# Four layers on one core: where a batch's last signs and its layer 3 stand among the next batch's scores

## The chip, the cores and the metric

The kernel runs on one core of a Trainium2 chip. The metric is the device time of one execution in microseconds (us). Three runs of the kernel before gave 1948.09, 1948.43 and 1948.29 us, median 1948.29. The profile is one more execution, of 1948.69 us, in which the engines' work spans 1946.8 us.

## The reference, cut to what matters

The input x has 8 batches of 512 channels and 32 x 32 = 1024 positions. Four layers follow one another, each with a residual.

```python
# layer 0: linear attention through 64 channels; sigma is a largest singular value
f, g = relu(batchnorm(Wf x)), relu(batchnorm(Wg x));  h = Wh x
x = Wv ((f^T g) / sigma  h^T) + x
# layer 1: group norm, softmax attention over 512 channels
h = group_norm(x);  a = softmax(q(h)^T k(h) / sqrt(512))
x = x + Wp (a v(h))
# layer 2: softmax attention over 128 channels
x = bn(Z (softmax(t(x)^T p(x) / sqrt(128)) g(x))) + x
# layer 3: product of signs
s = bn(sign(W) * scale @ sign(x + bias)) + x
out = prelu(s - shift) + bias
```

In layer 3 each batch's signs are a 512 x 1024 matrix of +1 and -1, multiplied by a 512 x 512 matrix of signs and then passed through a few elementwise operations.

## The kernel before, in words

**Stages.** A first section reads all batches for the batch norms of layer 0 and folds weights together; among them wu, so that u = wu h takes the place of q and k, and the scores of layer 1 are h^T u. Then `fast` (line 823) runs once for each batch, n = 0 to 7. A batch's 1024 positions are cut into two halves of 512 (`half`), its 512 channels into four chunks of 128 partitions. The steps of `fast` are:

1. `scores1`: the scores of layer 1 and their exponentials, in four rounds of seven products;
2. `make_v`: the values of layer 1, in two rounds of seven products;
3. `values1`: attention times values, 14 groups of products, added to x by GpSimd; on its way the next batch is normalised (`normal`, `split_h`);
4. `project2`, `scores2` and `values2`: layer 2. Between their products stand those of `make_u`, which makes the next batch's u, handed out one at a time by `fill`;
5. `close2` (line 654) for each half: layer 2's result is added to x by VectorE (L660);
6. `leave` (line 662) for each half: layer 3.

**Seven products.** The large products go through `seven` (line 318), a scheme that takes seven products of quarters instead of eight, with sums of quarters prepared beforehand. The factor on one side is cut into A11, A12, A21, A22 with sums S1 to S4, the other into B11 to B22 with T1 to T4. In the scores A is u and B the normalised batch h; S1, S2, S4 lie in the tile us, and S3 takes the place of A21 in ut. VectorE makes these sums when the last quarter of u is there (`sums_of`, lines 301 to 304: S1, S2, S3, S4 in this order). `seven` is a generator that stops after each product:

| stop | product | what follows it |
|---|---|---|
| 0 | A11·B11 into a bank pa | ACT copies it out (L335) |
| 1 | S2·T2 | VectorE adds the copy (L330) |
| 2 | S3·T3 | VectorE adds (L330) |
| 3 | S1·T1 into a bank pc | ACT copies it out (L324, or L326 with a bias), GpSimd adds (L345) |
| 4 | A12·B21 on top of pa | ACT moves it (L326), in the scores with exp (L351) |
| 5 | S4·B22 on top of pc | VectorE adds (L330, or L332 with a bias) |
| 6 | A22·T4 on top of S3·T3 | VectorE adds (L330, or L332 with a bias) |

`scores1` runs four such rounds, so its loop in `fast` counts k = 0 to 27; k = 0, 1, 2 are A11·B11, S2·T2, S3·T3 of the first round. Partial sums lie in eight PSUM banks that are handed round (`bank`).

**Layer 3.** `leave` does for a half: four signs on ACT (L668, one of 128 x 512 for each chunk, into the tile sg, fp16), then for j = 0 and 1 four products (L678) into a bank. The weights pack two sign matrices into one fp16 number, so ACT and VectorE take the result apart (L689, L690, L691). Then, for two outputs: L697 on VectorE adds x, L701 and L702 on ACT, L709 on VectorE, and SyncE sends 128 x 512 numbers out (L712). The generator stops after each j. The first half's `leave` runs in the same call of `fast`, with the next u's products in between. The second half's is put into the list `rest3` and taken up in the next batch's scores at odd k: at k = 1 the signs and j = 0, at k = 3 j = 1, at k = 5 its end, at which x of the batch after the next is asked for (`load_x`, L137) into the buffer that has become free.

**The chain.** `chain` (line 925) finds sigma for a pair of batches by repeated squaring of 128 x 128 matrices. Three such chains of 24 steps are spread behind the main work: `chore(2)` runs one step at every second stop of `scores1`, `make_v` and `values1`, so 14 + 7 + 7 steps in a batch, until all 72 are done, which is in n = 2. A step is two products (L938, L939) and their eviction, in turn by ACT (L952) and by VectorE; the steps of the latter kind also take a sum over partitions (L972) of the step before, which VectorE turns into a factor (L973, L999, L1000) before it evicts with that factor (L960) and prepares the next sum (L966, L967). A chain's end takes a logarithm and an exponential on ACT (L1010, L1013, each with a load of a table).

**What sets the order.** The program isn't executed in the order of the Python text. A scheduler in the layer that builds it orders the queue of each engine by the traced order, by what each instruction needs, and by costs that it assumes. In the built program of before, one of the two matmuls of A12·B21 stands in front of S2·T2, and the four signs of the second half stand on ACT behind L335 of the first round. Each engine then works through its queue in order.

Of the kernel before, what the change touches and what calls it, by code (L numbers as in the profile page):

```python
# [23 lines left out]
NH = N // HF  # L24
# [59 lines left out]
def kernel(  # L84
# [36 lines left out]
    def bank():  # L121
        return psum["bank"].tile([P, HF], F32, tag="bank", name="bank")
# [9 lines left out]
    def load_x(b, split=False):  # L132
        t = xpool.tile([P, CC, N], F32, tag="x", name="xt")
        src = x[b].rearrange("(cc p) n -> p cc n", p=P)
        for cc in range(CC):
            for ns in [half(h) for h in range(NH)] if split and not cc else [slice(0, N)]:
                nc.sync.dma_start(out=t[:, cc, ns], in_=src[:, cc, ns])  # L137
        return t

    def half(i):  # L140
        return bass.ts(i, HF)
# [73 lines left out]
    def col(name, i):  # L215
        return ct[:, COL[name] + i : COL[name] + i + 1]
# [234 lines left out]
    def split_h(env, ht):  # L451
        hs = env["big"].tile([P, 3, 2, HF], F32, tag="hs", name="hs")
        b = [ht[:, chunks[k], half(n)] for k in range(2) for n in range(2)]
        return differences_of(b, [hs[:, i] for i in range(3)])
# [199 lines left out]
    def close2(xt, att, h):  # L654

        for oc in range(CC):
            ps = bank()
            mm(out=ps, lhsT=sbw["z"][:, bass.ts(oc, P)], rhs=att, start=True, stop=True)  # L658
            xs = xt[:, oc, half(h)]
            nc.vector.tensor_tensor(xs, ps, xs, ALU.add)  # L660

    def leave(env, xt, dst, halves=range(NH), signs=None):

        small = env["small"]
        for h in halves:
            sg = env["e"].tile([P, CC, HF], F16, tag="e", name="sg")
            for cc in range(CC):
                nc.scalar.activation(  # L668
                    sg[:, cc, :], xt[:, cc, half(h)], AF.Sign, bias=rb3[:, cc : cc + 1]
                )  # L670
            for j in range(CC // 2):
                both = env["e"].tile([P, 2, HF], F32, tag="e", name="both")
                y1, y2 = both[:, 0, :], both[:, 1, :]

                def product(lt):
                    ps = bank()
                    for cc in range(CC):
                        mm(  # L678
                            out=ps,
                            lhsT=lt[:, cc, bass.ts(j, P)],  # L680
                            rhs=sg[:, cc, :],
                            start=cc == 0,
                            stop=cc == CC - 1,
                        )
                    return ps

                if signs is None:
                    ps = product(sw3)
                    nc.scalar.activation(y2, ps, AF.Identity, bias=round3, scale=1.0 / PACK)  # L689
                    nc.vector.tensor_scalar(y2, y2, ROUND, None, ALU.subtract)  # L690
                    nc.vector.scalar_tensor_tensor(y1, y2, -PACK, ps, ALU.mult, ALU.add)  # L691
                    sums = y1, y2
                else:
                    sums = [product(lt) for lt in signs]

                for y, ps, oc in ((y1, sums[0], j), (y2, sums[1], j + 2)):
                    nc.vector.scalar_tensor_tensor(  # L697
                        y, ps, sa3[:, oc : oc + 1], xt[:, oc, half(h)], ALU.mult, ALU.add
                    )
                    up = small.tile([P, HF], F32, tag="half_a", name="up3")  # L700
                    nc.scalar.activation(up, y, AF.Relu, bias=cb3[:, oc : oc + 1])  # L701
                    nc.scalar.activation(  # L702
                        y,
                        y,
                        AF.Identity,
                        bias=pb3[:, oc : oc + 1],
                        scale=col("L3_conv_pr_slope", oc),
                    )
                    nc.vector.scalar_tensor_tensor(  # L709
                        y, up, ps3[:, oc : oc + 1], y, ALU.mult, ALU.add  # L710
                    )
                    nc.sync.dma_start(out=dst[:, oc, half(h)], in_=y)  # L712
                yield
# [91 lines left out]
    def entering(n):  # L805

        b = order[n]
        f = load_f(b)

        def steps():  # L810
            while b // 2 not in ready:
                next(behind)
            if b % 2 == 0:
                for i in (b, b + 1):
                    pvs[i] = weights0(i)
            yield from enter(resident[b], f, pvs.pop(b))

        return steps()

    rest3 = []  # L820
    verdict = []

    def fast(env, n, hb, ua):


        b = order[n]
        xt = resident.pop(b)
        more = n + 1 < B
        ahead = iter(())
        count = [0]  # L830

        def chore(every):
            count[0] += 1
            if count[0] % every == 0:
                next(behind, None)

        es = [None] * NT
        for k, _ in enumerate(scores1(env, hb, ua, es)):
            if rest3 and k % 2:
                if next(rest3[0], "end") == "end":  # L840
                    rest3.pop()
                    if more and order[n + 1] not in resident:
                        resident[order[n + 1]] = load_x(order[n + 1])
            if k == 8 and more:
                ahead = entering(n + 1)
            if k >= 11 and k % 3 == 0:
                next(ahead, None)
            chore(2)
        for _ in ahead:
            pass  # L850
        esum = es.pop()
        vt = env["big"].tile([P, NT, C], F32, tag="uv", name="vt")
        for k, _ in enumerate(make_v(hb, vt)):
            if k == 3:
                r = inverse_sums(env, esum, n)
            chore(2)
        scratch = env["big"].tile([P, 3, N], F32, tag="us", name="scratch")
        got = []
        steps = iter(())
        for k, _ in enumerate(values1(env, xt, vt, es, r, scratch)):  # L860
            chore(2)
            if k == 5 and more:
                nxt = resident[order[n + 1]]
                hb = split_h(env, normal(env, nxt))
        signs = None
        if more:
            steps = make_u(env, hb, got)
        else:
            signs = unpacked(env)

        def fill(k=1):
            for _ in range(k):
                next(steps, None)

        made = []
        for k, _ in enumerate(project2(env, xt, made)):
            fill(k > 5)
        tt, pt, gt = made
        es, esum = scores2(env, pt, tt, lambda t: fill(t % 2))
        banks, r = [None, None], None  # L880

        def values2(h, ts):
            if banks[h] is None:
                banks[h] = bank()
            for t in ts:
                mm(  # L886
                    out=banks[h],
                    lhsT=gt[:, t, :],
                    rhs=es[t][:, half(h)],
                    start=t == 0,  # L890
                    stop=t == NT - 1,
                )
            if t == NT - 1:
                att = env["small"].tile([P, HF], F32, tag="half_b", name="att")
                nc.vector.tensor_tensor(att, banks[h], r[:, h, :], ALU.mult)
                return att

        dst = channels(out[b])  # L900
        fill()
        values2(0, range(0, 2))
        r = inverse_sums(env, esum, B + n)
        values2(0, range(2, NTH))
        att = values2(0, range(NTH, NT))
        values2(1, range(0, NTH))
        close2(xt, att, 0)
        att = values2(1, range(NTH, NT))
        count = iter(()) if more else count_bad(env)
        next(count, None)  # L910
        fill()
        for _ in leave(env, xt, dst, [0], signs):
            fill()
        close2(xt, att, 1)
        fill(2)
        for _ in steps:
            pass
        rest3.append(leave(env, xt, dst, [1], signs))
        if not more:
            for _ in rest3.pop():  # L920
                next(count, None)

        return hb, got[0] if more else None
# [111 lines left out]
    env = {}  # L1035
# [105 lines left out]
    for b in range(B):  # L1141
        xt = load_x(b) if b else first
# [361 lines left out]
    with tc.If(verdict[0] > 0):  # L1504
        with (
# [5 lines left out]
            env = {"big": big, "e": epool, "small": small}  # L1511
# [4 lines left out]
            for b in range(B):  # L1516
                xt = load_x(b)
# [43 lines left out]
```

## Time and profile before

| what | from the profile |
|---|---|
| span | 1946.8 us, of which the first section to the first u takes about 227 |
| one batch, scores to scores, n = 1 to 2 | 450.18 to 679.66 us |
| one batch, scores to scores, n = 3 to 4 | 900.67 us to 1113.09 us |
| matmul 128x512 fp32, two records | 0.86 us from one to the next |
| one sign product 128x512 fp16 | 0.21 us from one to the next |
| L668 sign on ACT | 0.72 us mean |
| chain of work that ended last | PE 93%, DVE 3%, ACT 2% |
| clock granted to TensorE | 0.997 |

In the lines of the page a product of fp32 is counted twice (its two passes), so x4 means two matmuls. A bracket at the end of a line of the time line gives the idle time of the engine before it and what ended it. PE's busy time overlaps from one matmul to the next, so the distance between two starts, not the duration, is what a matmul costs.

### The profile page before, as it was taken

The numbers are of one execution on the slowest core, as the hardware profiler recorded it, in microseconds if no ns is written. First come the engines' busy times: TensorE is split into PE (matmuls) and PEld (weight loads), VectorE is DVE, ScalarE is ACT, GpSimd is POOL, SyncE is SP. The second block draws the span as 40 slices with busy tenths as digits, with TensorE's granted clock in tenths as the row PEclk, the third lists the DMA queues.
The fourth block names the chain that finished last, engine by engine and source line by source line (L and its number), as shares of the span: only waits on it lengthen the run. The fifth ranks groups of instructions, "written<-read, shape, count | busy, mean of one in ns | idle before, by whom it ended". The sixth has DMA issues, their size and how long they took to land.

```text
span 1946.8 us, 16715 instructions
## 1 busy us (share of the span) xinstructions
PE 1908.0 (98%) x6230; PEld 982.9 (50%) x6230; DVE 1149.2 (59%) x1867; ACT 514.4 (26%) x815; POOL 223.6 (11%) x176
## 2 busy tenths in 40 slices
PE   8999999999999999999999999999999999999997
PEld 3367456544655446454555446544645455544653
DVE  3255577447864687537754677348663775466545
ACT  2141221134221342025212331034202421134014
POOL 1000001200112001200111011200120011101120
PEclk9999999999999999999999999999999999999999
DMA  8320000002000110002000120002000200010001
GB/s 322 147 76 7 1 6 12 1 11 87 17 1 0 33 65 17 1 8 85 17 5 1 33 71 12 1 11 87 11 0 1 73 26 10 0 33 22 11 0 56
DMA packets 27289, 67.00 MB, mean 34 GB/s; under 512 B 3824, under 2 KB 4592, under 8 KB 26560
## 3 DMA queue, kind: packets, MB, share of 16 engines
q1 hardware_dynamic: 26112, 65.09, 9.7%
q8 instruction: 51, 0.84, 0.2%
q0 software_dynamic: 224, 0.33, 0.1%
q10 hardware_dynamic: 864, 0.43, 0.1%
q14 instruction: 38, 0.31, 0.1%
HBM read 38.51 MB, written 18.87 MB: 29 GB/s over the span
## 4 chain that ended last, share of the span: by engine, by line
PE 93%; DVE 3%; ACT 2%; issue 0%; DMA 0%; ACTq 0%; POOL 0%; DVEq 0%
PE bank L373 43%; PE bank L540 20%; PE bank L886 6%; PE bank L764 6%; PE bank L1151 4%; PE bank L641 3%; PE bank L658 3%; PE bank L396 2%; PE wide L1191 1%; PE bank L678 1%; PE bank L938 1%; PE bank L939 1%; PE bank L785 1%; PE wide L1238 1%; DVE st L408 0%; ACT up L701 0%
## 5 line engine op out<-in xcount | busy, mean ns | idle before, releaser
L540 PE MATMUL bank<-e,vt 128*128 128x512 f32 x768 | 334.0, 593 | 0.0
L540 PEld LDWEIGHTS bank<-e,vt 128*128 128x128 f32 x768 | 145.0, 190 | 175.4 <-issue 173.2
L373 PE MATMUL bank<-ut,h 128*128 128x512 f32 x384 | 183.3, 598 | 4.7 <-ACT e L335 4.7
L330 DVE TENSOR_TENSOR e<-bank,e 128x512 f32<-128x512 f32 x128 | 87.7, 685 | 61.4 <-PE bank L373 60.2
L373 PE MATMUL bank<-us,hs 128*128 128x512 f32 x256 | 121.3, 596 | 0.5 <-DVE us L302 0.5
L373 PEld LDWEIGHTS bank<-ut,h 128*128 128x128 f32 x384 | 70.6, 190 | 87.7 <-issue 73.5
L886 PE MATMUL bank<-e,tpg 128*128 128x512 f32 x256 | 114.6, 595 | 0.0
L764 PE MATMUL bank<-tpg 128*128 128x512 f32 x256 | 114.6, 592 | 0.0
L771 ACT ACTIVATE e<-bank 128x512 f32<-128x512 f32 x128 | 76.4, 597 | 128.5 <-PE bank L764 128.5
L373 PE MATMUL bank<-h,wu 128*128 128x512 f32 x192 | 90.7, 594 | 2.2 <-ACT ut L335 1.5
L373 PE MATMUL bank<-wo,h 128*128 128x256 f32 x384 | 91.9, 382 | 0.0
L345 POOL TENSOR_TENSOR e<-e 128x512 f32<-128x512 f32 x32 | 41.6, 1300 | 432.3 <-ACT e L324 361.3
L776 DVE TENSOR_TENSOR esum<-esum,e 128x1024 f32<-128x1024 f32 x48 | 58.8, 1225 | 54.9 <-ACT e L771 54.9
L330 DVE TENSOR_TENSOR vt<-bank,vt 128x512 f32<-128x512 f32 x64 | 44.0, 688 | 69.5 <-PE bank L373 69.3
L886 PEld LDWEIGHTS bank<-e,tpg 128*128 128x128 f32 x256 | 48.0, 190 | 63.9 <-issue 63.9
L764 PEld LDWEIGHTS bank<-tpg 128*128 128x128 f32 x256 | 48.6, 190 | 60.8 <-issue 60.5
L373 PEld LDWEIGHTS bank<-wo,h 128*128 128x128 f32 x384 | 71.5, 190 | 14.3 <-ACT vt L324 4.9
L345 POOL TENSOR_TENSOR ut<-ut 128x512 f32<-128x512 f32 x16 | 21.8, 1360 | 483.0 <-ACT ut L326 483.0
L373 PEld LDWEIGHTS bank<-us,hs 128*128 128x128 f32 x256 | 47.3, 190 | 57.5 <-issue 51.4
L793 DVE RECIPROCAL rsum<-bank 128x512 f32<-128x512 f32 x16 | 53.7, 3356 | 30.3 <-PE bank L785 30.3
L668 ACT ACTIVATE sg<-xt,rb 128x512 f16<-128x512 f32 x64 | 43.8, 717 | 103.7 <-DVE xt L660 100.9
L1151 PE MATMUL bank<-xt,fg 128*64 128x512 f32 x256 | 59.3, 608 | 4.5 <-DMA fg<-in_w_fg 4.5
(320 smaller groups left out, 3076.3 us busy)
## 6 DMA issues: line engine op xcount, KB each, us to landing
xt<-in_x SPq DMA_DIRECT2D x55, 512.0 KB
out<-both SPq DMA_DIRECT2D x64, 256.0 KB
rfull<-rsum SPq DMA_DIRECT2D x64, 128.0 KB
f_dram<-f SPq DMA_DIRECT2D x8, 256.0 KB
fb<-f_dram SPq DMA_DIRECT2D x8, 256.0 KB
w<-in_w SPq DMA_DIRECT2D x1, 1024.0 KB
q<-in_w_q SPq DMA_DIRECT2D x1, 1024.0 KB
k<-in_w_k SPq DMA_DIRECT2D x1, 1024.0 KB
```

Source lines behind the costliest of these rows:

```text
L330: nc.vector.tensor_tensor(dst, ps, u, ALU.add)
L345: nc.gpsimd.tensor_tensor(c22, c22, c12, ALU.add)
L373: mm(out=ps[:, q * w : (q + 1) * w], lhsT=lt(ka, kb, q, k), rhs=rhs(ka, kb, q, k), start=first and q == 0 and k == 0, stop=last and k == 1 ...
L540: mm(out=ps, lhsT=a[:, t, bass.ts(r_, P)], rhs=e[t], start=first and t == 0, stop=last and t == NTH - 1, skip_group_check=True,)
L641: mm(out=ps[:, i, :], lhsT=xt[:, cc, bass.ts(4 * h + i, P)], rhs=sbw["tpg"][:, cc, 2 * P : 3 * P], start=cc == 0, stop=cc == CC - 1,)
L658: mm(out=ps, lhsT=sbw["z"][:, bass.ts(oc, P)], rhs=att, start=True, stop=True)
L764: mm(out=ps, lhsT=pt[:, 0, bass.ts(t, P)], rhs=tt[:, 0, half(h)], start=True, stop=True,)
L771: nc.scalar.activation(e[:, half(h)], ps, AF.Exp, scale=float(P) ** -0.5)
L776: nc.vector.tensor_tensor(esum, esum, e, ALU.add)
L793: nc.vector.reciprocal(r, ps)
L886: mm(out=banks[h], lhsT=gt[:, t, :], rhs=es[t][:, half(h)], start=t == 0, stop=t == NT - 1,)
L1151: mm(out=banks[i][side(h), :], lhsT=w0[i][:, cc, :], rhs=xt[:, cc, half(h)], start=cc == 0, stop=cc == CC - 1,)
```

## The change

`leave` gets an argument that makes it stop once more, after the signs. In `fast` the second half's `leave` is made before the last products of the next u are traced, and, if there is a next batch, its signs are traced there at once. In the next scores layer 3 is taken up at even k: j = 0 at k = 0, j = 1 at k = 2, its end (and `load_x`) at k = 4. As long as it runs, `chore` isn't called, so the two chain steps at k = 1 and k = 3 fall away there and all later steps come two later; this concerns n = 1 and n = 2 (in n = 0 there is no layer 3 left over, and from n = 3 on no chain).

```diff
-    def leave(env, xt, dst, halves=range(NH), signs=None):
+    def leave(env, xt, dst, halves=range(NH), signs=None, stop=False):
...
                     sg[:, cc, :], xt[:, cc, half(h)], AF.Sign, bias=rb3[:, cc : cc + 1]
                 )
+            if stop:
+                yield
             for j in range(CC // 2):
...
         for k, _ in enumerate(scores1(env, hb, ua, es)):
-            if rest3 and k % 2:
+            if rest3 and k % 2 == 0:
                 if next(rest3[0], "end") == "end":
                     rest3.pop()
...
-            chore(2)
+            if not rest3:
+                chore(2)
         for _ in ahead:
             pass
...
         close2(xt, att, 1)
+        rest3.append(leave(env, xt, dst, [1], signs, more))
+        if more:
+            next(rest3[0])
         fill(2)
         for _ in steps:
             pass
-        rest3.append(leave(env, xt, dst, [1], signs))
```

In the built program the queues hold the same instructions as before, in other places. At the start of the scores PE's queue reads A11·B11, the four sign products of j = 0, S2·T2, S3·T3, the four of j = 1, S1·T1, A12·B21; no half of A12·B21 is pulled ahead. On ACT the first of the four signs stands before the last L702 of the first half, two more before the last L326 of u, the fourth behind it and before L335. On SyncE the first transfer of x stands ahead of the two outputs of j = 1 and the second between them.

## The prediction

> **What bounds the kernel now.** I read the page first, then the list of who waited for whom on PE, then the time lines of PE, DVE and ACT around those waits. Batches are numbered n = 0 to 7 in the order they run.
>
> ```profile
> span 1946.8 us, 16715 instructions
> PE 1908.0 (98%) x6230; PEld 982.9 (50%) x6230; DVE 1149.2 (59%) x1867; ACT 514.4 (26%) x815; POOL 223.6 (11%) x176
> ```
>
> PE is busy for 98% and the granted clock is 9 tenths or more in every slice, so only idle PE time can be won. PE's waits in the whole span add up to some 26 us; two of the larger ones recur:
>
> ```profile
> PE bank L373 <- ACT e L335: 4.7, 7, 0.7
> PE bank L938 <- DVE cur L960: 3.9, 3, 1.8
> PE bank L416 <- DVE mv L415: 3.5, 5, 1.8
> ```
>
> (us in total, times, longest.) The first comes once in each of n = 1 to 7, the 1.8 us ones of the second once in n = 1 and once in n = 2. The third has one wait of 1.8 us before the main loop and four of 0.4 us late in the scores. Here is PE in n = 1, where the scores begin (start, duration):
>
> ```profile
> 450.18 1.88 PE L373 MATMUL bank<-ut,h 128*128 128x512 f32 x4
> 452.73 1.13 PE L373 MATMUL bank<-ut,h 128*128 128x512 f32 x2 [0.68 <-ACT e L335]
> 453.70 1.88 PE L373 MATMUL bank<-us,hs 128*128 128x512 f32 x4
> 455.41 1.03 PE L678 MATMUL bank<-sg,sw 128*128 128x512 f16 x4
> ```
>
> Every fp32 matmul is shown as two records. A pair (x4) is issued in 1.72 us elsewhere in this stage, four f16 products in 0.86. The first line is A11·B11; the second is half of A12·B21, pulled ahead while S2 isn't ready, and it must wait for ACT to copy A11·B11 out of the same bank. From 450.18 to the end of the sign products at 456.28 pass 6.10 us for 1.72 + 0.86 + 1.72 + 0.86 = 5.16 us of work: **0.94 us lost**, and n = 3 has the same 6.10 (900.67 to 906.77). What S2·T2 really needs is the second of DVE's sums:
>
> ```profile
> 449.96 1.23 DVE L301 TENSOR_TENSOR us<-ut 128x1024 f32<-128x1024 f32 x1
> 451.10 0.75 DVE L332 SCALAR_TENSOR_TENSOR ut<-bank,bu,ut 128x512 f32<-128x512 f32 x1
> 451.76 1.22 DVE L302 TENSOR_TENSOR us<-us,ut 128x1024 f32<-128x1024 f32 x1
> ```
>
> It ends at 452.98, 2.80 after 450.18. At n = 0, where nothing is pulled ahead, PE starts S2·T2 at 229.25, 0.05 after L302's end. ACT meanwhile:
>
> ```profile
> 446.05 0.81 ACT L702 ACTIVATE both<-both,pb,ct 128x512 f32<-128x512 f32 x1
> 446.95 0.69 ACT L326 ACTIVATE ut<-bank,bu 128x512 f32<-128x512 f32 x1
> 452.10 0.58 ACT L335 COPY e<-bank 128x512 f32<-128x512 f32 x1 [4.46 <-PE bank L373]
> 452.58 2.56 ACT L668 ACTIVATE sg<-xt,rb 128x512 f16<-128x512 f32 x4
> ```
>
> It idles 4.46 us, and the four signs come only afterwards. The second wait, in n = 1:
>
> ```profile
> 466.65 1.88 PE L373 MATMUL bank<-ut,h 128*128 128x512 f32 x4
> 470.34 0.46 PE L938 MATMUL bank<-cur 128*128 128x128 f32 x2 [1.81 <-DVE cur L960]
> ```
>
> ```profile
> 467.28 0.15 DVE L973 COPY tr<-bank 128x1 f32<-128x1 f32 x1
> ...
> 468.25 0.75 DVE L709 SCALAR_TENSOR_TENSOR both<-up,ps,both 128x512 f32<-128x512 f32 x1
> ...
> 469.65 0.54 DVE L960 TENSOR_SCALAR cur<-bank,r 128x256 f32<-128x256 f32 x1
> ```
>
> The chain's eviction L960 stands in DVE's queue behind layer 3's L690 to L709. PE was free at 466.65 + 1.72 = 468.37: 1.97 us idle, plus 0.07 for the slower restart (470.34 to 470.63 instead of 0.22): **2.04 us lost**, and the same in n = 2 (697.86 to 699.83).
>
> **What the Trainium skill says.** "PSUM — Partial Sum Buffer", Engine vs sequencer instructions: ACT, DVE and GpSimd queues are strict FIFO and matmuls start in program order. The trace agrees: L960 waits its turn above. Same page, PSUM bank collisions: a bank must not be written by PE while ACT reads it; agrees: PE goes on at 452.73, 0.05 after the copy's end at 452.68. "GPSIMD Engine Reference", Specifications: GpSimd shares SBUF interfaces with DVE instructions of two SBUF inputs or in a 2-port mode; agrees: L709, 0.74 alone, took 1.17 beside POOL's L345, and L690, 0.43 alone, 1.12. "ScalarE: Activation LUTs", What ACT_TABLE_LOAD costs: 1.283 us plus a drain of 1.38; the trace has 1.28 with the activation right behind (544.02, then 545.31), so 1.28 is used.
>
> **The change, part by part.** The queues of the built program show no instruction added or removed; only places change. T is the start of A11·B11.
>
> 1. Signs. ACT gets its four L668 (0.62 apart) before L335: the first before the last L702, two more before the last L326, the fourth after it. The x halves leave DVE's L660 at 445.73, 447.41, about 448.0 and 449.3. So sign 1 ends at 446.65, L702 at 447.35, signs 2 and 3 at 448.8, L326 at 449.4 (447.64 before), sign 4 at 450.0. Who is queued behind: L326, which the second matmul of A11·B11 (451.04) and L302 (451.76) need, and L709, which needs L702 and moves one L660 back on DVE. None is late, so DVE's L302 keeps 452.98. This costs nothing; ACT's 4.46 us gap hides it.
>
> 2. PE at the start of the scores. New order: A11·B11, sign products j=0, S2·T2, S3·T3, sign products j=1, S1·T1, A12·B21, and so on. Sign products run T+1.72 to T+2.58 (their bank is released by the second L332, 451.85 + 0.05 = T+1.72). S2·T2 starts at T+2.85. Loss 0.27 + 0.10 restart = 0.37 instead of 0.94: **gain 0.57, seven times: 4.0**. S3 (L303) is ready at T+3.98 and wanted at T+4.67. Bounds: 0.27 if the restart doubles and L302 slips 0.2; 0.67 if no restart cost shows.
>
> 3. Layer 3 behind it. DVE: L304 to T+5.08, L690, L330 of S2·T2, L691, L330 of S3·T3 (from T+6.66), L697 twice (first ends T+8.0), then L690, L691, L697 for j=1 to T+10.4. ACT: L689 twice (second ends T+8.14), L701 twice, L702 twice to T+10.9, L701 to T+11.5, then the copy L324 of S1·T1's bank to **T+12.0**. PE wants that bank for S4·B22 at T+2.85+1.82+1.72+0.86+1.72+1.72+1.72 = **T+12.4**; in n = 1 and 2 three chain matmuls (0.58) stand before it. It is just in time: cost 0, bound 0 to 0.4 a batch.
>
> 4. Chain. Steps at k = 1 and 3 of n = 1 and 2 fall away there and come later, four in all. Two products and one total run after A12·B21 (from T+10.74 in n = 1), when DVE has mostly done layer 3; its L960 then ends near T+14.8, and the next chain matmul stands at T+16.5, behind A22·T4, S4·B22 and the next A11·B11 (5.2 us of PE work; in n = 1 before it was 2.7). The stall goes: **2 x 2.04 = 4.1**. Bounds 0 (moved) to 4.1. Other steps keep their parity, so the 0.31 wait at 490.79 stays.
>
> 5. The moved steps. Their PE time is the same work elsewhere. In n = 1 the second chain now ends in the value stage: its trace sum must pass DVE's L446 x2, L330, L312, L562, L313, L563, L573 (0.66 to 1.5 each). From the stage's start V I get its L967 at V+6.8, PE wants it at V+6.9. I charge **0.2**; bounds 0 and 1. Two table loads (2.56) move onto ACT where it has only copies some 3 us apart; nobody on PE waits for these. POOL's L984 falls behind two L579 (5.05 for both) and holds DVE's L985 for up to 2 us; DVE idles 14 us of 50 in that stage and PE's operands for the next two groups are done. In n = 2 the third chain ends at the sixth step of the v stage, where the second did in n = 1 without a wait.
>
> 6. SP. x for the next batch is asked for at k = 4 instead of 5, its first transfer ahead of j=1's two outputs, the second between them. Before, loads started at T+15.9 (916.54) and DVE's first use at T+28.7 (929.40) waited for PE's bank, not for a transfer; the new last load is issued near T+16. Nothing.
>
> Sum: 4.0 + 4.1 - 0.2 = **7.9 us** of the 1946.8 us span: 1938.9. The timed runs lie 1.5 above this span (median 1948.29): **1940.4**.
>
> **Rivals.**
> (a) The chain stall moves instead of going: gain 4.0 - 0.2 = 3.8, 1944.5. For: the chain still crosses a busy DVE (POOL's L345 from T+12.1 slows L709 there). Against: 1.7 us of slack in step 4.
> (b) S4·B22 waits for L324, about 0.6 a batch, and eats the gain of step 2: 4.1 - 0.2 - 0.2 = 3.7, 1944.6. For: the margin is 0.4 us, on a sum of a dozen durations.
> (c) Slower: the same copy L324 is far late, because the L701 before it needs DVE's L690, L691, L697 of j=1, which stand behind j=0's. It decides from a wait of 7.9 / 7 = 1.1 us a batch, slower by 0.2% from 1.7; at 2.2 it gives 1940.4 + 15.4 = 1955.8. DVE would have to run 2.6 us later than I sum; nothing there takes that long, so it is unlikely.
> (d) No effect: the built queues exclude it.
>
> **How the numbers follow.** A measurement of this kernel can tell about 0.2% (3.9 us) from no change. Forecast 0.68 (its own range 1939.3 to 1942), (a) 0.14, (b) 0.14, (c) 0.04. (a) and (b) lie on the edge of 0.2%, half of each counts as faster: faster 0.81, same 0.15, slower 0.04. Range: down to 1939.0 (step 2 at 0.67, step 5 at 0: 8.8, with the runs' spread), up to 1944.4, just short of (a) and (b).
>
> **What would show it.** In the profile after: PE's wait for ACT L335 gone, replaced by some 0.3 us for DVE L302 seven times; ACT's L668 before L335; sign products right after A11·B11; no 1.81 us wait for L960; a wait for tj L967 in n = 1's value stage of 0.2 us. Wrong would be a wait of L373 for ACT e L324 near T+12, a wait for L960 near T+16, or L302 later than T+2.9.

## The result and the profile after

The changed kernel took 1939.49 us in the median of four runs (1938.61 to 1942.25), the kernel before 1948.19 in the median of four (1948.06 to 1948.43). The ratio is 0.9958, with a 95% interval of 0.994 to 0.9975: some 8.2 us faster by the ratio, 8.7 us between the medians. In the changed file the lines are 1 to 6 higher than before: the signs are L669, layer 3 is L681 and L692 to L712, the chain's products are L944 and L945, its eviction L966, its sum L978, and L973 gives tj.

The page's first lines, and from PE's list of waits (for whom: us in total, times, longest) the rows that answer to those shown above:

```profile
span 1940.4 us, 16698 instructions
...
PE 1909.5 (98%) x6230; PEld 984.6 (51%) x6230; DVE 1149.8 (59%) x1867; ACT 513.6 (26%) x815; POOL 224.1 (12%) x176
```

```profile
PE bank L416 <- DVE mv L415: 3.5, 5, 1.8
...
PE bank L373 <- DVE us L302: 0.5, 1, 0.5
...
PE bank L944 <- DVE cur L966: 0.3, 1, 0.3
```

The row of seven waits for the copy L335 is gone. Of the three waits for the chain's eviction only the one of 0.3 is left. The row for L302 is that of n = 0, as before. PE's time line in n = 1 (start, duration):

```profile
451.92 1.88 PE L373 MATMUL bank<-ut,h 128*128 128x512 f32 x4
453.63 1.03 PE L681 MATMUL bank<-sg,sw 128*128 128x512 f16 x4
454.77 1.98 PE L373 MATMUL bank<-us,hs 128*128 128x512 f32 x4
456.59 1.88 PE L373 MATMUL bank<-ut,h 128*128 128x512 f32 x4
...
464.13 1.88 PE L373 MATMUL bank<-us,h 128*128 128x512 f32 x4
...
468.43 0.39 PE L944 MATMUL bank<-cur 128*128 128x128 f32 x2
```

T is 451.92. The sign products end at 453.63 + 0.86 = 454.49, and S2·T2 starts at 454.77, T+2.85. The gap of 0.28 has no bracket, since the profile lets the sign products end at 454.66, only 0.11 before: so short a gap is seen only in the distance of the starts. S2·T2 then takes 1.82 to the next start instead of 1.72. The line at 464.13 is S4·B22, that at 468.43 the chain's next product, T+16.51, without a wait. ACT and DVE beside it:

```profile
447.67 0.71 ACT L669 ACTIVATE sg<-xt,rb 128x512 f16<-128x512 f32 x1
...
449.18 1.34 ACT L669 ACTIVATE sg<-xt,rb 128x512 f16<-128x512 f32 x2
450.43 0.67 ACT L326 ACTIVATE ut<-bank,bu 128x512 f32<-128x512 f32 x1
451.04 0.72 ACT L669 ACTIVATE sg<-xt,rb 128x512 f16<-128x512 f32 x1
...
463.21 0.56 ACT L324 COPY e<-bank 128x512 f32<-128x512 f32 x1
```

```profile
453.50 1.22 DVE L302 TENSOR_TENSOR us<-us,ut 128x1024 f32<-128x1024 f32 x1
...
466.14 0.54 DVE L966 TENSOR_SCALAR cur<-bank,r 128x256 f32<-128x256 f32 x1
467.20 0.74 DVE L712 SCALAR_TENSOR_TENSOR both<-up,ps,both 128x512 f32<-128x512 f32 x1
```

The signs are done at 451.76, before T. L302 ends at 454.72, T+2.80, where it ended before. L324 ends at T+11.85, 0.36 ahead of S4·B22. L966 ends at T+14.76.

**How the runs are compared.** Up to S2·T2 of n = 0, PE's first product that waits for L302 in the main loop, both kernels do the same. That section ended at 229.25 in the profile of before and at 230.99 in that of after, so the two spans hide 1.74 us (the last section returns to this). Below, the time from there to the end of the span is called the window. The span is given to 0.1 us, so a window is good to 0.05. The distance between the L302 of one batch and the next gives the batches:

| kernel | gate on chain steps | signs | layer 3 at k | window | n = 1 | n = 2 | n = 3 |
|---|---|---|---|---|---|---|---|
| before | no | behind | odd | 1717.55 | 229.49 | 221.01 | 212.42 |
| after | yes | ahead | even | 1709.41 | 225.92 | 219.52 | 211.86 |
| e1 | yes | behind | odd | 1715.78 | 226.31 | 222.40 | 212.43 |
| e2 | yes | ahead | odd | 1715.74 | 226.31 | 222.40 | 212.42 |
| e3 | yes | behind | even | 1713.45 | 226.46 | 220.09 | 212.41 |
| e4 | no | ahead | even | 1709.51 | 226.87 | 218.40 | 211.86 |
| e5 | no | behind | even | 1716.10 | 228.79 | 220.31 | 212.42 |

A window comes from one profiled execution each. The batches of kernels with the same order agree within 0.02 (n = 3 of before, e1, e2, e3 and e5), so in a batch a difference of a tenth can be read. A window is coarser: the stretch from VectorE's last result to the end of the span, in which the last results are sent out, takes 5.1 to 5.5 us over these profiles, also where the order is the same (5.2 in after, 5.4 in e4, which are alike from n = 3 on). After's window is 8.14 shorter than before's: n = 1 and 2 together 5.06, n = 3 to 6 by 0.56 to 0.60 each, and what follows the L302 of n = 7 by some 0.8, of which 0.3 lies behind VectorE's last result (5.4 in before). Without that 0.3 the gain is 7.9. Where chain steps move between n = 1 and n = 2, only their sum counts. The run times are coarser still: in the later series the kernel before took between 1945.88 and 1952.34 us, so the narrow range of its first four runs is no measure of the noise.

### The profile page after: what moved, and what is told of

Read it like the earlier page. It is cut to its first block, busy times and chain, and to the rows that moved or that the text cites. A ratio compares the mean times of both kernels' runs of the same rounds, so it can differ in the third digit from the quotient of the medians.

```text
span 1940.4 us, 16698 instructions
## 1 busy us (share of the span) xinstructions
PE 1909.5 (98%) x6230; PEld 984.6 (51%) x6230; DVE 1149.8 (59%) x1867; ACT 513.6 (26%) x815; POOL 224.1 (12%) x176
## 4 chain that ended last, share of the span: by engine, by line
PE 89%; DVE 8%; ACT 1%; issue 1%; DMA 0%; ACTq 0%; POOL 0%; DVEq 0%
PE bank L373 40%; PE bank L540 20%; PE bank L890 6%; PE bank L767 6%; PE bank L1157 4%; PE bank L641 3%; PE bank L396 2%; PE bank L658 1%; PE wide L1197 1%; PE bank L944 1%; DVE both L712 1%; DVE both L700 1%; PE bank L945 1%; PE bank L788 1%; PE wide L1244 1%
## 5 line engine op out<-in xcount | busy, mean ns | idle before, releaser
L330 DVE TENSOR_TENSOR e<-bank,e 128x512 f32<-128x512 f32 x128 | 87.7, 685 | 65.2 <-PE bank L373 64.5
L330 DVE TENSOR_TENSOR vt<-bank,vt 128x512 f32<-128x512 f32 x64 | 44.1, 689 | 70.5 <-PE bank L373 70.1
L669 ACT ACTIVATE sg<-xt,rb 128x512 f16<-128x512 f32 x64 | 45.2, 718 | 104.4 <-DVE xt L660 100.9
```

What stands on the lines that cost most here:

```text
L330: nc.vector.tensor_tensor(dst, ps, u, ALU.add)
L669: nc.scalar.activation(sg[:, cc, :], xt[:, cc, half(h)], AF.Sign, bias=rb3[:, cc : cc + 1])
```

## The experiments

**Which part gives what: e1 to e5.** The change has three edits: the gate (no chain step while layer 3 is pending), the signs traced ahead, and layer 3 at even k. Each ratio below is to the kernel before, with its 95% interval; differences of windows are to before where no other kernel is named. The signs ahead alone weren't run. e1 is the kernel before with the gate alone:

```diff
-            chore(2)
+            if not rest3:
+                chore(2)
```

> Only the gate on the chain steps: signs and layer 3 stay where they are before the change (signs behind the copy L335, layer 3 at odd k). By the theory on record the two parts of the gain are separate: the boundary loss of 0.94 us stays in n = 1 to 7 (the seven waits of PE for ACT's L335, 4.7 us together, are still in the list), the two 1.8 us waits for the chain's eviction are gone, 4.1 - 0.2 = 3.9 us: about 1944.3 against 1948.2. Rival (the stall only moves to the next chain matmul): within 1 us of 1948.2.

Measured: ratio 0.9988 (0.9981 to 0.9995), window 1.77 shorter. The seven waits for L335 are all there, as expected, but the chain gave 1.8 and not 3.9. Three smaller waits have come in; the first in n = 1, the others later in n = 2:

```profile
468.97 0.46 PE L939 MATMUL bank<-cur 128*128 128x128 f32 x2 [0.36 <-DVE cur L961]
...
745.81 0.46 PE L939 MATMUL bank<-cur 128*128 128x128 f32 x2 [0.42 <-DVE cur L961]
...
772.97 0.35 PE L973 MATMUL bank<-tj,mask 128*128 128x1 f32 x2 [0.56 <-DVE tj L968]
```

With their restarts they come to some 2.0 us, while the wait of 0.31 that before has at 490.79 is gone; the rest of the 2.1 that are missing isn't assigned. So with the gate alone the two waits of 1.8 are gone, but in n = 1 the eviction still stands behind layer 3's last result (0.36), and other waits have come in. This is not quite the gate of the change either: at odd k layer 3 is pending until k = 5, so the first chain step of a batch comes at k = 6. From the L302 of n = 1 to the next, 24 chain evictions are executed, against 27 in before and 25 in after, and n = 2 begins with one by ACT where before and after have one by VectorE.

e2 is the changed kernel with one edit undone:

```diff
-            if rest3 and k % 2 == 0:
+            if rest3 and k % 2:
```

> The signs ahead and the gate, but layer 3 still at odd k. In the built queue PE again has half of A12*B21 and then S2*T2 in front of the sign products, as before the change. If the boundary gain needs the sign products in front of S2*T2 (the theory), the loss there stays 0.94 and the gain is the chain's alone, 3.9: 1944.3. If ACT's signs standing behind the copy were the cause by themselves (rival), the gain is 7.9: 1940.3.

Measured: ratio 0.9987 (0.998 to 0.9994), window 1715.74, the same as e1 to 0.04, with the same waits and the same longer gate. Signs ahead are worth nothing as long as half of A12·B21 and S2·T2 stand in front of the sign products.

e3 is the changed kernel with the signs left where they were (the lines that put `leave` into `rest3` as before, no `next` there).

> Layer 3 at even k and the gate, but the signs not ahead: they stand behind the copy L335 on ACT. Theory: the sign products now have to wait for signs that end at about T+3.2, 3.8, 4.4 and 5.1 (T the start of A11*B11; in the trace of before the copy ends at T+2.5 and signs follow 0.62 apart), PE has 5.16 us of work to do until then and 0.2 of products behind the last sign; loss 0.9 to 1.2, so nothing is gained at the boundary: 3.9 or a little less, 1944.3 to 1946. Rival (even k alone is enough): 7.9, 1940.3.

Measured: ratio 0.9981 (0.9973 to 0.9989), window 4.10 shorter. The boundary loses what it lost before (212.41 in n = 3), the sign products now standing among S2·T2's matmuls, behind the wait for L335 as before; the chain's 1.8 us waits are gone. With e2, this shows that signs ahead and even k give the boundary's gain only together.

e4 is the changed kernel without the gate:

```diff
-            if not rest3:
-                chore(2)
+            chore(2)
```

> Everything of the change except the gate: the chain steps stay at k = 1 and 3. The step on record credits the chain's 4.1 us to the steps that fall away; then the 1.8 us waits stay and the gain is 4.0: 1944.2. Rival, which the built queue of VectorE speaks for: with layer 3 at even k the chain's eviction stands in front of the last layer-3 results, at about T+9.5 by a sum of durations, and PE has the next chain product only near T+11; then the stall goes without the gate and the gain is about 8: 1940.2.

Measured: ratio 0.9954 (0.994 to 0.9967), window 1709.51. This is the whole gain without the gate, so the rival is right. n = 1 and 2 together take 445.27, 0.17 less than in after. DVE in n = 1 (T = 449.52), and PE there:

```profile
458.71 0.54 DVE L965 TENSOR_SCALAR cur<-bank,r 128x256 f32<-128x256 f32 x1
459.16 0.75 DVE L712 SCALAR_TENSOR_TENSOR both<-up,ps,both 128x512 f32<-128x512 f32 x1
...
464.50 0.54 DVE L965 TENSOR_SCALAR cur<-bank,r 128x256 f32<-128x256 f32 x1
464.96 1.40 DVE L712 SCALAR_TENSOR_TENSOR both<-up,ps,both 128x512 f32<-128x512 f32 x2
```

```profile
460.02 0.39 PE L943 MATMUL bank<-cur 128*128 128x128 f32 x2
...
467.14 0.39 PE L943 MATMUL bank<-cur 128*128 128x128 f32 x2
```

Both evictions go in front of layer-3 results, and PE comes for them at 460.02 and 467.14, 0.8 and 2.1 us after they end.

e5 is the kernel before with layer 3 at even k alone (the edit of e2 the other way round), to see whether even k is the whole cause.

> The kernel before with one edit: layer 3 of the second half at even k; no gate, signs behind the copy. Theory formed from the earlier runs (the gate gives nothing; even k alone takes the chain's stall away; the boundary needs signs ahead and even k together): the two 1.8 us waits are gone, the seven 0.7 us waits for L335 stay, the time from S2*T2 of n = 0 to the end falls by 4.1 us from 1717.55 to about 1713.4, a little under the run with the gate (1713.45). Rival (the gate is needed as long as the signs stand behind): 1715.5 to 1717.5.

Measured: ratio 0.9996 (0.9988 to 1.0005), window only 1.45 shorter. By its run times it can't be told from before. The theory written for it falls, and the window lies where the rival has it: half of the stall is still there, in n = 1 and again in n = 2.

```profile
471.59 0.46 PE L938 MATMUL bank<-cur 128*128 128x128 f32 x2 [0.93 <-DVE cur L960]
```

What orders these runs is when the chain's last eviction among layer 3 gets through DVE, against when PE is free for it (n = 1, from T, from the time lines):

| kernel | last layer-3 result on DVE ends | eviction ends | PE free for the next product |
|---|---|---|---|
| before | 19.55 | 20.01 | 18.19 |
| e5 | 18.86 | 19.31 | 18.37 |
| e1, e2 | 18.72 | 19.17 | 18.80 |
| e3 | 17.51 | 16.25 | 17.07 |
| e4 | 16.84 | 15.52 | 17.62 |
| after | 16.02 | 14.76 | 16.51 |

In the first three rows the eviction stands behind the last result of layer 3 (L709 in before), ends 0.45 after it, and is late. In the other three layer 3 is through 2.0 to 3.5 us earlier than in before, and the eviction goes in front of its last result. These three have even k in common, with the gate (e3), with the signs ahead (e4) or with both (after); even k alone isn't enough (e5). Beside the other two edits the gate makes no difference that a window can tell (1709.41 with it, 1709.51 without).

**The margin of L324: e8.** In the changed kernel two activations of layer 3 are executed twice, with the same values:

```diff
                     nc.scalar.activation(up, y, AF.Relu, bias=cb3[:, oc : oc + 1])
+                    if stop and j == 0:
+                        nc.scalar.activation(up, y, AF.Relu, bias=cb3[:, oc : oc + 1])
```

> The changed kernel with two of layer 3's ACT instructions (L704 of j = 0) executed twice, 0.6 us each, in front of the copy L324: about 1.2 us more ACT work ahead of it than the 0.4 us margin that the prediction gave. In the built queue PE's S4*B22 moves behind the next round's first product or products (1.7 to 5 us later). If the order of PE's queue takes the delay up (theory): no wait for L324 and 1709.4 +- 0.3 from S2*T2 of n = 0 to the end. If the margin is hard (rivals b and c): a wait of up to 0.8 us a batch, 7 x 0.8 = 5.6, 1712 to 1715.

Measured: ratio 0.9961 (0.9945 to 0.9976), window 1709.45, 0.04 more than after, which is no difference. ACT and PE in n = 1 (T = 450.29):

```profile
464.82 0.57 ACT L324 COPY e<-bank 128x512 f32<-128x512 f32 x1
465.28 0.59 ACT L351 ACTIVATE e<-bank 128x512 f32<-128x512 f32 x1
```

```profile
463.36 1.88 PE L373 MATMUL bank<-ut,h 128*128 128x512 f32 x4
...
465.52 1.90 PE L373 MATMUL bank<-us,h 128*128 128x512 f32 x4
```

L324 ends at T+15.10, 3.25 later than in after, because more of layer 3 now stands in front of it too. The scheduler has put the next round's A11·B11 (463.36) ahead of S4·B22 (465.52), which again finds the copy 0.13 before. The 0.4 us of the prediction are a margin for one fixed order; the program that is built with a slower ACT has another order.

**Filling the last 0.37 us: e6, e7, e9 to e12.** In e6 the changed kernel takes both groups of sign products ahead of S2·T2; e7 is the same without the gate.

```diff
+            if k == 0 and rest3:
+                next(rest3[0])
             if rest3 and k % 2 == 0:
```

> The changed kernel with the sign products of j = 1 pulled in front of S2*T2 too, to fill the 0.27 us that PE still waits there for VectorE's L302 (0.37 lost with the restart). On ACT the copy L324 of S1*T1's bank then stands behind all of layer 3's eight L704 and L705, some 2 us of work more; the built queue puts S4*B22 of n = 3 and later behind the next round's A11*B11 (1.7 us later). Theory: S2*T2 starts at T+3.45 instead of T+2.85, no loss there, 7 x 0.37 = 2.6 gained: 1706.8 from S2*T2 of n = 0 to the end instead of 1709.41, against the kernel before 1937.5. Rival (b, c of the prediction): PE waits for L324 in front of S4*B22, 0.4 us a batch or more, and the time is that of the changed kernel or above it.

> As the run before, and without the gate on the chain steps. If both are right (0.37 a batch filled, the gate worth -0.1 to -0.2): 1706.7 from S2*T2 of n = 0 to the end. If the chain's eviction L966 now meets layer 3's work, which comes earlier and denser on VectorE, a wait of PE for L966 of 0.5 to 2 us shows in n = 1 and 2, and the time is above that of the run with the gate: 1707.5 to 1710.

Measured: e6 0.9977 (0.9969 to 0.9984), window 1712.35; e7 0.9976 (0.9966 to 0.9986), window 1711.51. By the windows both are longer than after, by 2.9 and 2.1 us, and e7 lies above the range that was given for it. The gap is filled, S2·T2 starts at T+3.44, and PE doesn't wait for L324, but in e6 n = 3 gains only 0.08 over after, n = 1 loses 2.5 and n = 2 0.8. DVE and PE of e6 in n = 3, then PE in n = 1:

```profile
907.86 2.73 DVE L700 SCALAR_TENSOR_TENSOR both<-both,sa,xt 128x512 f32<-128x512 f32 x4
...
912.43 0.68 DVE L330 TENSOR_TENSOR e<-bank,e 128x512 f32<-128x512 f32 x1
```

```profile
909.59 3.60 PE L373 MATMUL bank<-ut,h 128*128 128x512 f32 x8
913.26 1.95 PE L373 MATMUL bank<-ut,hs 128*128 128x512 f32 x4
...
464.54 1.96 PE L373 MATMUL bank<-ut,hs 128*128 128x512 f32 x4 [1.11 <-DVE tr L981]
```

DVE runs all four L700 in one piece, and the additions L330 of S2·T2 and S3·T3 come behind them. A22·T4 goes on top of S3·T3's bank and waits until that L330 has read it (913.11): PE is free at 909.59 + 3.44 = 913.03, starts at 913.26 and takes 1.79, so 0.30 of the 0.37 is lost again. In n = 1, where the profile names L981 that follows the L330 on DVE, it is 1.11, and in n = 2 1.33. Neither theory named this wait.

e9 takes only two of the four products of j = 1 ahead, so that DVE gets nothing earlier; e10 is e9 without the gate.

```diff
-                    ps = product(sw3)
+                    if stop and j == 1:
+                        ps = product(sw3, ccs=range(2, CC), ps=part)
+                    else:
+                        ps = product(sw3)
+                    if stop and j == 0:
+                        part = product(sw3, 1, range(2))
```

> The changed kernel with the first two of j = 1's four sign products taken in front of S2*T2, the other two left behind S3*T3; VectorE's part of j = 1 can start no earlier than before. S2*T2 then starts at T+3.01 instead of T+2.85 with 0.43 us of work done that came later before: 0.37 a batch less lost, 7 x 0.37 = 2.6, so 1706.8 from S2*T2 of n = 0 to the end instead of 1709.41, against the kernel before 0.9945. Rival: the built queue now has S4*B22 straight behind A12*B21, at T+10.3, where the run without the gate had the copy L324 end at T+10.6 (460.12 after 449.52): a wait of about 0.3 takes the place of the one removed, 1708.9 to 1709.6.

> As the run before, without the gate on the chain steps: n = 1 and 2 have a chain step in front of S4*B22 and so more room for the copy L324. Theory: as the run before, 0.1 to 0.2 less: 1706.7 if the gap is filled, 1708.8 to 1709.5 if L324 is waited for from n = 3 on; no wait for the chain's eviction above 0.31.

Measured: e9 0.9956 (0.9943 to 0.997), window 1709.23; e10 0.996 (0.9946 to 0.9974), window 1708.64. The rival is right for e9. e10 waits for L324 from n = 3 on too, and lies a little under the range given for that. PE and ACT of e9 in n = 3:

```profile
905.85 1.88 PE L373 MATMUL bank<-ut,h 128*128 128x512 f32 x4
907.82 1.98 PE L373 MATMUL bank<-us,h 128*128 128x512 f32 x4
909.64 1.88 PE L373 MATMUL bank<-ut,hs 128*128 128x512 f32 x4
```

```profile
907.20 0.56 ACT L324 COPY e<-bank 128x512 f32<-128x512 f32 x1
```

S4·B22 could start at 907.57 and starts at 907.82, after L324 ends at 907.76; with the slower restart (1.82) 0.35 is lost. This is rival (b) of the prediction, in another kernel.

e11 is e10 with one chain step traced ahead of n = 0's scores (`next(behind, None)` before the loop where n == 0).

> As the run before, with one chain step traced in front of n = 0's scores. In n = 0 PE waits 0.53 us for L302 in front of S2*T2; a chain step is 0.45 to 0.58 us of PE work whose operands are ready. If it fills that wait: 0.5 us less than the run before. If the shift of all later chain steps by one brings a wait for the chain's eviction elsewhere (in 1 of 24 steps a wait of 0.3 stands now): the same or up to 2 us more. The time from n = 0's A11*B11 is compared, since the step lies before S2*T2.

Measured: ratio 0.9987 (0.9981 to 0.9994). The wait of n = 0 is filled, but all later chain steps change places: PE now waits twice for tj, 1.6 at the longest, twice 0.6 for the eviction and twice 0.6 for r_r (L228). From the chain step or A11·B11 of n = 0 to the end it takes 1945.0 - 228.64 = 1716.36, e10 1937.2 - 226.15 = 1711.05: 5.3 more, where up to 2 had been expected.

e12 is e10 with A22·T4 in front of S4·B22 in the first round of the scores:

```diff
+        if swap:
+            term(pd, "A22", "T4", False, True)
+            yield
         term(pc, "S4", "B22", False, True)
```

> As the run with two sign products ahead and no gate, and in the first round of the scores A22*T4 goes in front of S4*B22, with VectorE's two additions in the old order behind them. The copy L324 then has 1.72 us more before PE wants its bank; it was late by 0.25 (S4*B22 at 907.82 after 905.85 + 1.72 = 907.57 in n = 3). Theory (L324 is the wait that took the gap's place): S4*B22 doesn't wait, 7 x 0.35 = 2.4 us less from n = 3's kind of batch: 5 x 0.35 = 1.8 for n = 3 to 7 and up to 0.7 in n = 1 and 2, so 1706.2 to 1706.9 from S2*T2 of n = 0 to the end instead of 1708.64, a batch of n = 3 at 211.47 instead of 211.83. Rival: A22*T4 waits in turn for VectorE's L330 of S3*T3 (as when both sign groups were ahead, 0.3 a batch), 1708.3 to 1709.

Measured: ratio 0.9955 (0.9941 to 0.9968), window 1706.67, n = 3 in 211.47, as the theory has it. PE in n = 3:

```profile
894.69 1.46 PE L686 MATMUL bank<-sg,sw 128*128 128x512 f16 x6
895.98 1.88 PE L377 MATMUL bank<-us,hs 128*128 128x512 f32 x4
...
903.28 1.88 PE L377 MATMUL bank<-ut,hs 128*128 128x512 f32 x4
905.00 1.88 PE L377 MATMUL bank<-us,h 128*128 128x512 f32 x4
```

Every start follows the one before by the work alone. By the window e12 is 2.0 us shorter than e10 and 2.7 us shorter than the changed kernel. By the run times (median 1939.56, 1935.97 to 1940.77) the two can't be told apart: their intervals are almost the same, and runs of one kernel differ by more than 2.7.

## Why the prediction was right, and where it was not

The forecast of 7.9 us stands against 8.14 in the window, or 7.9 without what lies behind VectorE's last result, and 1940.4 against a median of 1939.49. That the two times agree to 1 us is partly luck: the first section alone varies by 3.8 us between executions.

1. **Signs** (cost 0): right. They fill ACT's idle time and L302 keeps T+2.80.
2. **PE's order at the start of the scores** (0.57 a batch): right in size and cause. S2·T2 starts at T+2.85, the restart costs 0.10, and n = 3 is 0.56 shorter. e2 and e3 show that signs and even k are both needed. The wait for L302 was to appear in the list seven times and doesn't; by the profile's ends it is 0.11, too short to be listed.
3. **L324 just in time** (cost 0): right, T+11.85 against 12.0. In n = 1 the margin is 0.36, since one matmul of A22·T4 goes behind S4·B22; in n = 3 S4·B22 starts at T+12.41, as said. The bound of 0.4 a batch, and rival (c), took the order of PE's queue as fixed, and e8 shows that the scheduler moves it.
4. **Chain** (4.1): right in size. n = 1 and 2 together gain 5.06, of which 2 x 0.56 is the boundary's, so 3.94 with the 0.2 of step 5 taken off. The path was right too: the eviction ends at T+14.76 and the next chain product stands at T+16.51, against 14.8 and 16.5. What was wrong is what the step credits, the chain steps that fall away at k = 1 and 3. With them in place the stall is gone as well (e4: 5.23 - 2 x 0.56 = 4.11), and the gate alone, in its longer form, gives 1.8 (e1). What replaces that sentence: even k with the signs ahead brings layer 3 through DVE 2.7 to 3.5 us earlier than before, with the gate or without it, and the eviction no longer stands behind its end.
5. **The moved steps** (0.2): right. The chain's end, in PE's and DVE's time lines of n = 1's value stage, V = 545.71:

```profile
545.71 7.11 PE L540 MATMUL bank<-e,vt 128*128 128x512 f32 x16
552.74 0.35 PE L978 MATMUL bank<-tj,mask 128*128 128x1 f32 x2
552.95 3.25 PE L540 MATMUL bank<-e,vt 128*128 128x512 f32 x7
```

```profile
552.30 0.29 DVE L973 TENSOR_REDUCE tj<-diag 128x1 f32<-128x128 f32 x1
```

   tj ends at V+6.88, PE starts L978 at V+7.03. From 545.71 to 552.95 pass 7.24 for eight matmuls (6.87) and one L978 (0.15): 0.22 lost. It agrees with e4, which moves no chain step and takes 0.17 less in n = 1 and 2.
6. **SP** (nothing): right; in PE's list transfers are waited for in the first section only.

Of the rivals, (a) didn't come: the next chain product has 1.75 us to spare. (b) and (c) didn't either, though e9 is what (b) looks like. (d) is excluded by the result.

## What to carry to other kernels

A wait in an in-order queue is cured by moving what stands in front of it or by moving the waiter; try the edits of a change one by one, alone and left out, since here the gate was worth nothing in company of the other two, and the boundary's gain came only with both of these. Look at what an edit does in its new company, too: at odd k the same gate held one stop longer. Before filling a gap on the busiest engine, follow each bank that the pulled-ahead work brings forward to the product that needs it next: the gap came back as a wait of nearly its own size in front of A22·T4 (0.30 of 0.37) and then of S4·B22 (0.35). Where a scheduler builds the queues, read the built order of every variant, because a margin in one order says little of the next.

## What the runs showed of the hardware that was not expected

PE's first products run at half speed for a time that differs from one execution to the next. The same 4 and 8 records, in the profile of before and then of after:

```profile
10.11 1.08 PE L1151 MATMUL bank<-xt,h 128*64 128x512 f32 x4 [1.31 <-DMA h<-in_w_h]
11.02 1.89 PE L1151 MATMUL bank<-xt,fg 128*64 128x512 f32 x8
```

```profile
10.02 1.98 PE L1157 MATMUL bank<-xt,h 128*64 128x512 f32 x4 [1.37 <-DMA h<-in_w_h]
11.78 2.89 PE L1157 MATMUL bank<-xt,fg 128*64 128x512 f32 x8
```

The first has the later rate from 10.11 on, the second only within the line at 11.78: by the next line it is 1.77 us behind (14.50 against 12.73), and it stays so. The views of the granted clock give 1.00 in both in these 20 us, but they count time without a record as full clock: the first record of the clock in the trace starts at 9.01 us in before and at 13.79 in after, where the starts of after's products go from 0.85 to 0.43 apart. The Trainium skill, "TensorE: Matmul & The Clock Gate", Part 1: The HAM clock gate, says that the array starts at half its clock and is let go after a window of some 3.4 us of work, and that the window runs free, so that the number of slow matmuls differs between runs. The traces agree on the half rate and on the difference; here the slow part lasted longer than 3.4 us, from the first product at 4.4 to before 10.1 in one and into the line at 11.78 in the other, with a wait of 1.3 us for h inside. Half rate comes back later in the same section: in before the granted clock is 0.50 from 183.1 to 186.5 us, and L1191's products start 0.85 us apart instead of 0.43; in e12 and e8 it is 1.00 there. The page hides this, since one of its slices is 49 us long. Over the profiles the section up to S2·T2 of n = 0 ended between 227.53 (e12) and 231.35, with the first transfers' waits (0.5 to 2.3 us for h) as another part that varies. That is as much as the forecast's parts, and so a sum of parts has to be tested from a point behind it.
